# A three-layer graph network: layer 2's twelve dense blocks in three teams of four instead of four teams of three

## The chip, the cores and the metric

The kernel runs on one core of one Trainium2 chip. The time is the device time of one execution in microseconds; the median of three executions of the kernel before is 1999.56 us (1996.38 to 2002.89). All views come from one further execution that the hardware profiler recorded.

## The reference

A graph of 6250 nodes and 100,000 edges, with a self-loop at every node, goes through three graph convolutions (256 to 512, 512 to 512, 512 to 256 columns), each followed by a relu; the result is added to the input and normalized by rows.

```python
deg = segment_sum(ones, dst)              # with the self-loops
norm_edge = rsqrt(deg)[src] * rsqrt(deg)[dst]
for W, b in ((W1, b1), (W2, b2), (W3, b3)):
    msg = (h @ W)[src] * norm_edge[:, None]
    h = relu(segment_sum(msg, dst) + b)
out = layernorm(x + h)
```

## The kernel before

The nodes are cut into 50 blocks of 125 (`Q`). The edges come sorted by destination, so each block has one run of about 2000 edges. Layer by layer the kernel forms, for each block, the sum of its neighbours' rows (a table in HBM: `tables[i]`), multiplies by the weights, and stores its rows of the next table. A block's sum is formed in one of two ways.

- **Gathered** (`gather`, L1198, and `product`, L1226): GpSimd (POOL) issues 16 indirect DMAs, each of 128 rows (in layer 2 of 512 floats, 256 KB), and one more for each group of ten blocks. VectorE makes one-hot matrices, and 26 matmuls add the rows up in a PSUM bank of `accs` (`sacc`). The rows land in a ring of row buffers; a buffer is free again when the block's sum has used it.
- **Dense**: small integers count how often each source occurs for each destination (`kept`, one byte each). ScalarE (ACT) turns five 125x125 pieces at a time into floats (L969 for teams, L1179 elsewhere), and TensorE (PE) multiplies them with all 50 blocks of the table (L1017 for teams).

In layer 2 blocks 0 to 11 are dense and 12 to 49 gathered. The dense ones go in **teams** (`teams`): a team's blocks share every load of the table. A unit is one table block for one team: two units come by one load (L82 by `load`, a pair of DMAs of 448 and 52 KB into one of three `streamed` buffers, in the profile `parts<-tab`); ACT writes the rounded half (L977) and VectorE (DVE) the rest (L979) into one of three `both_parts`; then PE does two matmuls (one pair) for each member of the team, each member in a PSUM bank of its own (`team_banks`). Teams begin at the end of layer 1, and fill the gap in which layer 2's gathers wait for the last rows of its table.

All of this is one program order, written at build time. For layer 2 the loop over gathers (612 of them, counted as `chunk` in `layer`) issues one gather, then the product that has become due (5 gathers behind its block's last), and then lets every generator that is due go one step. A team's generator does one pair for a step. A finished sum goes through `after2`: DVE scales the bank and adds the block's own row (L1367; the own row is loaded by SyncE's queue, SP, and scaled by ACT at L1238), PE transposes the result into the same bank (L1300), ACT copies it out to `zt2` (L1387), and the bank is free. In the order that copy stands eight gathers behind the sum, and the next block's sum eight gathers behind the copy. Two blocks together then go through W2 (L1413, with ACT's relu at L1424) and W3 (L1433). A team's sum is scaled into a `team_sums` buffer first (L1374) and transposed later into another bank (L1393, copied at L1396); where it can, such a block forms a couple with a gathered one.

All engines work in order. The ring of layer 2 has 30 rows: 10 in `room` (13 less one for each `team_sums` buffer), 14 in pairs, 8 on loan from the place of layer 3's table (two for each of `LOANED`), less two that are set aside. When the teams have 12 units left (`RETURN`), loaned rows are no longer used, and the ring has 22.

PSUM has eight banks. Layer 2 uses `accs[0]` and `accs[1]` in turn for gathered sums, `accs[2]`, `mat_ps` and `smm` for the team, `win_ps` and `str` for everything else, and one for constants.

Of the kernel before, what the change touches and what calls it, by code (L numbers as in the profile page):

```python
# [38 lines left out]
PRODUCTS = sum(c1 - c0 for c0, c1 in WINDOWS)  # L39
RUNS = 8  # L40

LOANED = 4
RETURN = 12
LAG = 5
FIRST_ROWS = 20
# [14 lines left out]
FRONT = 12  # L60
FRONT_AT = 3
EXTRA = 4
TEAM = 3
TEAMS = 4
HOME = 19
MANY = 29
ALONE = 2
# [8 lines left out]
def by_rows(queue, tile_rows, dram_rows, store=False):  # L76

    for s in (slice(0, EVEN), slice(EVEN, Q)):
        if store:
            queue.dma_start(out=dram_rows[s], in_=tile_rows[s])  # L80
        else:
            queue.dma_start(out=tile_rows[s], in_=dram_rows[s])  # L82
# [320 lines left out]
def sorted_path(ctx: ExitStack, tc: tile.TileContext, x, edges, starts, found, wts, biases, room, late, again, out):  # L403
# [42 lines left out]
    mat_bank = ps_mat.tile([P, HID], F32, name="mat_ps")  # L446
    win_bank = ps_mat.tile([P, HID], F32, name="win_ps")
# [8 lines left out]
    held, idle = {}, {}  # L456
# [6 lines left out]
    def take(name, most):  # L463
        while held.get(name, 0) >= most:
            yield 1
        held[name] = held.get(name, 0) + 1
# [309 lines left out]
    wide_rows = [room[:, at:at + HID] for at in range(MW, room.shape[1] - 2 * pair - HID + 1, HID)]  # L776
    team_sums = [wide_rows.pop()[:Q] for _ in range(TEAM)]
    last_rows = [room[:, at:at + C] for at in range(3 * MW, room.shape[1] - C + 1, C)]
# [27 lines left out]
    accs = [ps_sum.tile([P, HID], F32, name=f"sacc{n}") for n in range(3)]  # L806
    mm_bank = ps_sum.tile([P, HID], F32, name="smm")
# [116 lines left out]
    def carved(words):  # L924
        nonlocal cut
        cut += words
        assert cut <= tail.shape[1]
        return tail[:, cut - words:cut]

    RING = 3  # L930
    carved(LOANED * 2 * HID)
    loaned = [wide_tail[:, cut - n * HID:][:, :HID].bitcast(F32) for n in range(2 * LOANED, 0, -1)]
    is_loaned = {id(row) for row in loaned}
    streamed = [carved(2 * HID).bitcast(F32).rearrange("p (b c) -> p b c", b=2) for _ in range(RING)]
    both_parts = [carved(2 * HID) for _ in range(3)]
    on_loan = set()
    team_used = [[carved(-(-2 * PIECE * Q // 4)).bitcast(U8)[:, :2 * PIECE * Q].rearrange("p (k v) -> p k v", v=Q) for _ in range(TEAM)]
                 for _ in range(2)]
    team_pieces = [[carved(PIECE * Q).rearrange("p (k v) -> p k v", v=Q) for _ in range(TEAM)] for _ in range(2)]
    team_banks = [accs[2], mat_bank, mm_bank]  # L940
    couple, waiting = [], []
    teams_done = False
    returning = None
# [1 line left out]
    def teams(groups):  # L945
# [4 lines left out]
        def used_by(g, c):  # L950
            return team_used[(g * CUTS // 2 + c // 2) % 2]
# [5 lines left out]
        def next_counts(g, c):  # L957
            if c + 2 < CUTS:
                fetch_counts(g, c + 2)
            elif g + 1 < len(groups):  # L960
                fetch_counts(g + 1, c + 2 - CUTS)
# [6 lines left out]
        def piece(g, c, n):  # L968
            nc.scalar.copy(team_pieces[(g * CUTS + c) % 2][n], used_by(g, c)[n][:, c % 2 * PIECE:(c % 2 + 1) * PIECE, :])  # L969
            if c % 2 and n == TEAM - 1:  # L970
                next_counts(g, c - 1 + 2)
# [15 lines left out]
        yield 14  # L987
        for n in range(TEAM):
            piece(0, 0, n)
# [99 lines left out]
    def layer(i, width, gathered, dense, after, rows, first=0, spacing=1.0, extras=(), filler=None):  # L1089
# [8 lines left out]
        going = []  # L1098
        fixed = [[at, steps] for at, steps in extras]
        idle.clear()  # L1100
        idle.update(acc=accs[:2] if i == 1 else list(accs), acc_d=[mm_bank, win_bank, mat_bank])
        if i == 0:
            del idle["acc"]
        items = []
# [6 lines left out]
        acc_d = None  # L1111
        if done:
            acc_d = idle["acc_d"].pop(0)
# [13 lines left out]
        def go(chunk):  # L1127
            for item in list(going):
                if item[0] <= chunk + late:
                    wait = next(item[1], None)  # L1130
                    if wait is None:
                        going.remove(item)
                    else:
                        item[0] = chunk + late + min(wait, item[2])

        def need(chunk, name, most):
            nonlocal late
            while held.get(name, 0) >= most:
                late += 1
                go(chunk)  # L1140
            held[name] = held.get(name, 0) + 1

        def sum_bank(name, most):
            nonlocal late
            if i == 0:
                while not common:
                    if early_copy[0]():
                        break
                    late += 1
                    go(chunk)  # L1150
                return common.popleft()
            need(now, name, most)
            return idle[name].pop(0)

        def ended(chunk, b, acc, bank="acc"):

            most = LATE if chunk < total - 2 * KF else 1
            going.append([chunk + late + min((3, SOON, LATE)[i], most), after(b, acc, bank), most])
            for item in going:
                item[2] = most  # L1160
# [4 lines left out]
        def one_hot(b):  # L1165

            hot = hots[b] = onehot.tile([P, PRODUCTS, WIN], F32, name="shot")
            at = 0
            for w, (c0, c1) in enumerate(WINDOWS):
                shape = [P, c1 - c0, WIN]  # L1170
                nc.vector.tensor_tensor(hot[:, at:at + c1 - c0], near_cols[:, w * WIN:(w + 1) * WIN].unsqueeze(1).to_broadcast(shape),
                                        dlo[:, b, c0:c1].unsqueeze(2).to_broadcast(shape), op=ALU.is_equal)
                at += c1 - c0
# [27 lines left out]
        def product(c):  # L1201
            n, b, j = items[c]
            if b is None:
                return
            if j == 2:
                one_hot(b)
            if j == KF - LATE:
                if i == 0 and b >= OWN_FROM:
                    by_rows(nc.sync, own_x[b % 2], tables[0][b * Q:(b + 1) * Q, :])
                if i == 1:  # L1210
                    by_rows(nc.sync, own_row, tables[1][b * Q:(b + 1) * Q, :])
            if j < KF - 1:
                return
            acc = sum_bank("acc", 2 if i == 1 else 3)
            own_product = i == 2 or i == 0 and b < OWN_FROM
            if own_product:
                for h in range(2):
                    nc.tensor.matmul(acc[:, :C], lhsT=ident_r[:Q], rhs=parts[:, b, h * C:(h + 1) * C], start=(h == 0), stop=False)
            hot = hots.pop(b)
            of = [landed.pop((b, k)) for k in range(KF)]  # L1220
            each = of + [of_ten[b // GRP]]
            for k in range(max(c1 - c0 for c0, c1 in WINDOWS)):
                at = k
                for w, (c0, c1) in enumerate(WINDOWS):
                    if c0 + k < c1:
                        nc.tensor.matmul(acc[w * WIN:(w + 1) * WIN, :width], lhsT=hot[:, at], rhs=each[c0 + k],  # L1226
                                         start=(not own_product and k == 0), stop=(c0 + k == c1 - 1))
                    at += c1 - c0
            for row in of:
                if id(row) in is_loaned:  # L1230
                    on_loan.discard(id(row))
                    if returning is not None:
                        continue
                ring.append(row)
            if i == 0 and b >= OWN_FROM:
                nc.scalar.activation(own_x[b % 2], own_x[b % 2], AF.Copy, scale=dinv[:, b:b + 1])
            if i == 1:
                nc.scalar.activation(own_row, own_row, AF.Copy, scale=dinv[:, b:b + 1])  # L1238
            ended(now, b, acc)
# [3 lines left out]
        with tc.manual_schedule():  # L1243
            to_sum = 0
            for chunk in range(total + LAG):
# [18 lines left out]
                while done < until:  # L1264
                    m, k = divmod(done, NB)
                    if k == 0:
# [3 lines left out]
                        acc_d = sum_bank(bank, 3)  # L1270
# [89 lines left out]
    def after2(b, acc, bank):  # L1360
# [10 lines left out]
        else:  # L1371
            yield from take(f"sum{b % TEAM}", 1)
            zs = team_sums[b % TEAM]
            nc.vector.tensor_scalar(zs, acc[:Q], dinv[:, b:b + 1], None, op0=ALU.mult)  # L1374
            free(bank, acc)
            if b >= TEAM * (TEAMS - 1) and acc is not mm_bank:
                wins.append(acc)
            yield SOON
            while now < steps(TEAM * TEAMS) - 2 * KF and (len(couple) != 1 or held.get("turn", 0)):
                yield 1  # L1380
# [27 lines left out]
        for f2 in range(0, KH, each):  # L1408
# [11 lines left out]
            for _ in range(2):  # L1420
                if now < steps(TEAM * TEAMS) - 4 * KF and held.get("acc", 0) < 2 and not any(held.get(f"sum{t}", 0) for t in range(TEAM)):
                    yield 1
# [135 lines left out]

    team_work = teams([every[g * TEAM:(g + 1) * TEAM] for g in range(TEAMS)])
    first = 16  # L1560
# [5 lines left out]
    def last_weights():  # L1566
# [11 lines left out]
    own_row = two.enter_context(tc.tile_pool(name="sown_row", bufs=1)).tile([P, HID], F32, name="own_row")[:Q]  # L1578
    gap = (steps(TEAM * TEAMS) - 100) // (MANY - FEW - EXTRA)
    layer(1, HID, every[TEAM * TEAMS:], [], after2, wide_rows,  # L1580
          extras=[(5, last_weights()), (0, team_work), (20, home())]
# [197 lines left out]
```

## Time and profile before

| | |
|---|---|
| median of 3 executions | 1999.56 us |
| profiled execution, its span | 2010.4 us, 2008.7 us |
| PE, POOL, DVE, ACT busy | 92%, 69%, 45%, 45% of the span |
| first to last gather of layer 2 | 703.5 to 1540.2 us |
| mean of DMA traffic | 217 GB/s over the span |

A matmul counts twice in the trace where the type makes the hardware pass twice. Matmuls overlap, so a PE that is busy is not yet a PE at its peak: paces are read from the starts of successive matmuls. In a row of groups, the part behind the bar is busy us, mean ns of one, then idle time before them and what ended it. The chain of waits gives start, length and what the time went to; a DMA in it counts from its issue to its landing.

### The profile page before, as it was taken

What the parts mean: (1) busy time and instruction counts of PE and PEld (TensorE: products, weight loads), DVE (VectorE), ACT (ScalarE), POOL (GpSimd) and SP (SyncE); (2) the same over time, 40 slices, a digit from 0 to 9 for tenths busy, and PEclk for the clock granted to TensorE, in tenths of its full rate; (3) what the DMA queues carried; (4) which work ended last, traced back from release to release, by engine and by line L of the source; (5) the groups of instructions that cost most, each with busy time, mean ns of one, the idle gap of its engine ahead of it and who ended that gap; (6) DMA issues with size and microseconds to landing.
All of it is one profiled execution on the core that took longest, in us unless ns stands there. A gap on an engine that the chain in (4) does not pass through costs nothing.

```text
span 2008.7 us, 31171 instructions
## 1 busy us (share of the span) xinstructions
PE 1848.8 (92%) x11066; PEld 1251.0 (62%) x11066; DVE 901.2 (45%) x1901; ACT 897.8 (45%) x1614; POOL 1380.0 (69%) x1442
## 2 busy tenths in 40 slices
PE   3389999999998969999999999999988999999996
PEld 2367677667674535666666666666644767677773
DVE  4887777666666323323243223432311334343443
ACT  0677677777775423443243433343212333333331
POOL 2277777677677476777777677775775677777775
PEclk9999999999999989999999999999999999999997
DMA  7555555455559899999999999999986576666663
GB/s 162 168 148 175 154 172 155 149 159 173 152 162 253 214 284 267 297 295 284 294 294 280 290 282 289 290 287 266 279 247 196 138 191 181 190 189 190 187 184 109
DMA packets 197012, 435.75 MB, mean 217 GB/s; under 512 B 44124, under 2 KB 87814, under 8 KB 196845
## 3 DMA queue, kind: packets, MB, share of 16 engines
q0 software_dynamic: 88128, 265.01, 46.0%
q1 hardware_dynamic: 92749, 156.71, 28.5%
q10 hardware_dynamic: 15968, 11.92, 2.4%
q8 instruction: 89, 1.46, 0.3%
q14 instruction: 78, 0.64, 0.1%
HBM read 378.83 MB, written 54.66 MB: 216 GB/s over the span
## 4 chain that ended last, share of the span: by engine, by line
PE 73%; DMA 13%; DVE 4%; issue 3%; ACT 2%; POOL 1%; SPq 1%; ACTq 0%; DVEq 0%; POOLq 0%
PE sacc L1226 13%; PE mat_ps L1279 8%; PE sacc L1279 7%; PE win_ps L1279 7%; PE smm L1279 6%; PE win_ps L1413 4%; DMA own_row<-tab 4%; DMA parts<-tab 3%; PE sacc L1017 3%; PE mat_ps L1017 3%; PE smm L1017 3%; DMA row<-tab,ssrc 2%; PE win_ps L1433 2%; PE str L1413 2%; DMA parts<-kept 2%
## 5 line engine op out<-in xcount | busy, mean ns | idle before, releaser
L1198 POOL DMA_INDIRECT row<-tab,ssrc x780 | 754.1, 967 | 273.6 <-issue 162.1
L1198 POOL DMA_INDIRECT room<-tab,ssrc x484 | 467.6, 966 | 174.0 <-issue 97.7
L1179 ACT CAST piece<-room 125x625 fp32r<-125x625 uint8 x416 | 299.8, 728 | 250.9 <-PE mat_ps L1279 76.2
L1226 PE MATMUL sacc<-row,shot 128*32 128x512 f32 (+1 forms) x1786 | 290.4, 510 | 20.9 <-DMA row<-tab,ssrc 17.6
L1226 PE MATMUL sacc<-room,shot 128*32 128x256 f32 (+1 forms) x1506 | 278.6, 489 | 21.9 <-DMA room<-tab,ssrc 21.5
L833 DVE TENSOR_TENSOR room<-near_cols,slots 128x625 bf16<-128x625 f32 (+2 forms) x390 | 289.6, 802 | 11.9 <-PE sacc L905 7.7
L979 DVE TENSOR_TENSOR parts<-parts 125x512 fp32r<-125x512 f32 x200 | 136.4, 690 | 332.6 <-ACT parts L977 306.8
L977 ACT CAST parts<-parts 125x512 fp32r<-125x512 f32 x200 | 121.8, 620 | 165.5 <-DMA parts<-tab 78.3
L1279 PE MATMUL sacc<-parts,piece 125*125 125x512 f32 x600 | 186.3, 428 | 0.0
L1279 PE MATMUL mat_ps<-parts,piece 125*125 125x512 f32 x700 | 185.0, 406 | 0.0
L1226 PEld LDWEIGHTS sacc<-row,shot 128*32 128x32 f32 x1786 | 86.1, 111 | 133.0 <-issue 74.8
L1017 PE MATMUL sacc<-parts 125*125 125x512 f32 x400 | 145.5, 440 | 18.4 <-ACT parts L977 14.8
L1279 PE MATMUL smm<-parts,piece 125*125 125x512 f32 x605 | 156.7, 405 | 2.7 <-ACT piece L1179 2.1
L1198 POOL DMA_INDIRECT parts<-tab,ssrc x128 | 126.0, 984 | 47.6 <-issue 26.8
L1279 PE MATMUL win_ps<-parts,piece 125*125 125x512 f32 x600 | 150.2, 400 | 0.0
L1226 PEld LDWEIGHTS sacc<-room,shot 128*32 128x32 f32 x1506 | 84.5, 112 | 103.8 <-issue 50.3
L1179 DVE CAST piece<-room 125x625 fp32r<-125x625 uint8 x85 | 43.4, 511 | 229.5 <-PE smm L1279 75.5
L1279 PEld LDWEIGHTS mat_ps<-parts,piece 125*125 125x125 f32 x700 | 123.8, 186 | 31.8 <-issue 6.5
L1017 PE MATMUL smm<-parts 125*125 125x512 f32 x400 | 138.5, 428 | 0.3 <-ACT room L867 0.3
L1017 PE MATMUL mat_ps<-parts 125*125 125x512 f32 x400 | 138.5, 428 | 0.0
L905 PEld LDWEIGHTS <-room 128*125 128x125 bf16 x650 | 88.1, 140 | 79.5 <-issue 27.9
L1367 DVE SCALAR_TENSOR_TENSOR szs<-sacc,sdinv,own_row 125x512 f32<-125x512 f32 x38 | 28.5, 750 | 231.1 <-PE sacc L1226 143.6
(358 smaller groups left out, 2975.0 us busy)
## 6 DMA issues: line engine op xcount, KB each, us to landing
parts<-tab SPq DMA_DIRECT2D x105, 448.0 KB
kept<-room SPq DMA_DIRECT2D x29, 683.6 KB
room<-kept SPq DMA_DIRECT2D x29, 683.6 KB
tab<-st SPq DMA_DIRECT2D x62, 224.0 KB
row<-tab,ssrc POOLq DMA_INDIRECT x780
own_row<-tab SPq DMA_DIRECT2D x38, 224.0 KB
parts<-kept SPq DMA_DIRECT2D x60, 136.7 KB
room<-tab,ssrc POOLq DMA_INDIRECT x484
```

Of the source, the lines that this page charges most:

```text
L833: nc.vector.tensor_tensor(out, near_cols[:, :shape[2]].unsqueeze(1).to_broadcast(shape), numbers.unsqueeze(2).to_broadcast(shape), op=ALU. ...
L905: nc.tensor.matmul(bank[:Q, len(pair) * 256:][:, :G * NB], lhsT=hot_lo, rhs=hot_key, start=True, stop=True)
L977: nc.scalar.copy(to[:, :HID], row)
L979: nc.vector.tensor_sub(to[:, HID:], row, to[:, :HID].bitcast(F32))
L1017: nc.tensor.matmul(team_banks[n][:Q], lhsT=team_pieces[(g * CUTS + k // PIECE) % 2][n][:, k % PIECE, :], rhs=both_parts[u % 3][:, h * HID: ...
L1179: convert(piece, made_or_read[:, c * PIECE:(c + 1) * PIECE, :])
L1198: nc.gpsimd.indirect_dma_start(out=row, out_offset=None, in_=tables[i], in_offset=bass.IndirectOffsetOnAxis(ap=at, axis=0))
L1226: nc.tensor.matmul(acc[w * WIN:(w + 1) * WIN, :width], lhsT=hot[:, at], rhs=each[c0 + k], start=(not own_product and k == 0), stop=(c0 + k ...
L1279: nc.tensor.matmul(acc_d[:Q], lhsT=got[done // PIECE][:, k % PIECE, :], rhs=parts[:, k], start=(k == 0), stop=(k == NB - 1))
L1367: nc.vector.scalar_tensor_tensor(zs, acc[:Q], dinv[:, b:b + 1], own_row, op0=ALU.mult, op1=ALU.add)
L1413: nc.tensor.matmul(h_ps[:, f, :], lhsT=w2_sb[:, k, (f2 + f) * P:(f2 + f + 1) * P], rhs=zt2[:, k, :wide], start=(k == 0), stop=(k == KH - 1))
L1433: nc.tensor.matmul(u_ps[:, h, :], lhsT=ht2[:, k, h * Q:(h + 1) * Q], rhs=w3_sb[:, k, :], start=(k == 0), stop=(k == KH - 1))
```

## The change

Four numbers and two lists change. `TEAM` and `TEAMS` go from 3 and 4 to 4 and 3, so the same twelve blocks are dense. The team's fourth bank is `accs[1]`, so gathered sums have `accs[0]` alone. The second pair of `team_pieces` and `team_used` buffers that a fourth member needs comes from the room that `LOANED` = 2 instead of 4 sets free, four rows of the ring; and a fourth `team_sums` buffer takes one more. The ring has 25 rows, and 21 when the loan is returned.

```diff
-LOANED = 4
+LOANED = 2
-TEAM = 3
-TEAMS = 4
+TEAM = 4
+TEAMS = 3
@@ sorted_path
-    team_banks = [accs[2], mat_bank, mm_bank]
+    team_banks = [accs[1], accs[2], mat_bank, mm_bank]
@@ layer
-        idle.update(acc=accs[:2] if i == 1 else list(accs), acc_d=[mm_bank, win_bank, mat_bank])
+        idle.update(acc=accs[:1] if i == 1 else list(accs), acc_d=[mm_bank, win_bank, mat_bank])
@@ product, in layer
-            acc = sum_bank("acc", 2 if i == 1 else 3)
+            acc = sum_bank("acc", 1 if i == 1 else 3)
```

Up to the third gathered sum of layer 2, PE's order is the same in kind. Behind the fourth (block 15) it differs. On PE, from the end of that sum on, before the change (`sacc_934` to `sacc_936` are the three `accs`; `room` at L1393 is a team's sum; L905 are matmuls that count for layer 3):

```order
L1017 MATMUL sacc_936<-parts 125x512 x2
L1017 MATMUL mat_ps<-parts 125x512 x2
L1393 MATMUL win_ps<-ident_r,room 128x125 x4
L1017 MATMUL smm<-parts 125x512 x2
L1017 MATMUL sacc_936<-parts 125x512 x2
L905 LDWEIGHTS hot_pair_6533
L905 MATMUL str<-hot_pair_6533 125x250
L1300 MATMUL sacc_935<-ident_r,szs 128x125 x4
L1017 MATMUL mat_ps<-parts 125x512 x2
L905 LDWEIGHTS hot_pair_6533
L905 MATMUL str<-hot_pair_6533 125x250
L1017 MATMUL smm<-parts 125x512 x2
```

And with the change:

```order
L1017 MATMUL mat_ps<-parts 125x512 x2
L1017 MATMUL smm<-parts 125x512 x2
L1017 MATMUL sacc_935<-parts 125x512 x2
L1017 MATMUL sacc_936<-parts 125x512 x2
L905 LDWEIGHTS hot_pair_6517
L905 MATMUL str<-hot_pair_6517 125x250
L1300 MATMUL sacc_934<-ident_r,szs 128x125 x4
L1017 MATMUL mat_ps<-parts 125x512 x2
L905 LDWEIGHTS hot_pair_6517
L905 MATMUL str<-hot_pair_6517 125x250
L1017 MATMUL smm<-parts 125x512 x2
L1017 MATMUL sacc_935<-parts 125x512 x2
```

A unit now has four pairs, in four banks, and the first team, which ended before this place, ends some 50 gathers later: its transposes (L1393) are gone from here, and so are those of W2's runs that belonged to them. Up to the fifth sum there are 16 pairs in both; instructions of L1413 are 16 before and 8 now, of L1393 8 and none.

On ACT, from the copy of the same block's transposes on, before:

```order
L1387 COPY room<-sacc_935 128x4x125
L867 CAST room<-str 125x2x50x5
L1424 ACTIVATE room<-win_ps,b_sb 128x250 x2
L977 CAST parts<-parts 125x512
L1238 ACTIVATE own_row<-own_row,sdinv 125x512
L1396 COPY room<-win_ps 128x4x125
L977 CAST parts<-parts 125x512
L867 CAST room<-str 125x2x50x5
L977 CAST parts<-parts 125x512
```

And with the change:

```order
L1387 COPY room<-sacc_934 128x4x125
L977 CAST parts<-parts 125x512
L867 CAST room<-str 125x2x50x5
L977 CAST parts<-parts 125x512
L1424 ACTIVATE room<-win_ps,b_sb 128x250 x2
L1238 ACTIVATE own_row<-own_row,sdinv 125x512
L977 CAST parts<-parts 125x512
L969 CAST parts<-parts 125x625 x2
L867 CAST room<-str 125x2x50x5
```

The copy of the team's transposes (L1396) is gone from here, the copy at the head reads the one bank that gathered sums now have (`sacc_934`, before `sacc_935` in turn with it), and the scaling of the next own row (L1238) stands behind it, and ahead of the next copy, as before.

## The prediction

> **What bounds the kernel now.** I read stages first, then what each engine waits for, then the chain. The first view is the busy time of the engines by stage of layer 2 (columns: window, its length, then busy us and count of PE, PEld, DVE, ACT, POOL, then the granted clock, the DMA share and GB/s).
>
> ```profile
> 703.00:760.00 57.00, 40.35 (x172) 19.23 (x174) 11.45 (x22) 14.79 (x26) 42.25 (x43) 0.85 1.00 283
> 760.00:827.00 67.00, 60.99 (x327) 39.99 (x320) 26.14 (x46) 24.27 (x46) 45.62 (x49) 0.97 1.04 276
> 827.00:1403.00 576.00, 566.02 (x3223) 372.43 (x3226) 186.86 (x354) 216.76 (x401) 408.11 (x416) 0.99 1.03 288
> 1403.00:1541.00 138.00, 126.28 (x750) 73.15 (x747) 32.84 (x72) 30.14 (x64) 104.02 (x106) 0.98 0.85 252
> 1541.00:2008.00 467.00, 437.20 (x2650) 317.81 (x2642) 174.86 (x501) 157.08 (x261) 326.66 (x339) 0.96 0.63 172
> ```
>
> In 827 to 1403 both PE (566 of 576 us) and the DMA engines (1.03) look full, so I ask which one waits. Busy time of matmuls overlaps, so I count them: the next four rows are that stretch for line 1017 (the teams' matmuls), 1226 (sums over gathered rows), 1413 (W2) and 1433 (W3), in this order; then come their paces, two rows of PE's timeline and four of the chain of waits, and the longest of six rows of PE's waits there (total, times, longest us).
>
> ```profile
> 827.00:1403.00 576.00, 251.77 (x838) 150.03 (x838) 0.99 1.03 288
> 827.00:1403.00 576.00, 163.83 (x1356) 44.34 (x1360) 0.99 1.03 288
> 827.00:1403.00 576.00, 126.83 (x544) 101.44 (x544) 0.99 1.03 288
> 827.00:1403.00 576.00, 68.26 (x288) 53.45 (x288) 0.99 1.03 288
> 869.22 0.63 PE L1017 MATMUL mat_ps<-parts 125*125 125x512 f32 x2
> 869.68 0.62 PE L1017 MATMUL smm<-parts 125*125 125x512 f32 x2
> 850.38 6.14 PE sacc L1226 x52
> 933.38 1.69 PE win_ps L1413 x8
> 834.47 1.73 PE win_ps L1433 x8
> 1402.93 6.14 PE sacc L1226 x52
> PE sacc L1017 <- ACT parts L977: 6.4, 3, 3.4
> ```
>
> A pair of team matmuls starts every 0.46 us (869.22, 869.68): 838/2 x 0.46 = 193. A gathered block's sum has 52 records in 6.14: 1356/52 x 6.14 = 160. Eight records of W2 take 1.69: 544/8 x 1.69 = 115; of W3 1.73: 288/8 x 1.73 = 62. Together 530 us, without the transposes and the counting matmuls; and the waits that the last row heads come to 9.9 us (6.4, 1.5, 0.8, 0.5, 0.5, 0.2) of 576. **PE is the bound from 827 to 1403**, and the change takes nothing from it there. POOL confirms it: it waits for PE.
>
> ```profile
> L1198 POOL DMA_INDIRECT row<-tab,ssrc x196 | 193.6, 988 | 76.2 <-issue 39.6 <-PE sacc L1226 25.6 <-DMA room<-tab,ssrc 4.0
> 1404.18 0.94 POOL L1198 DMA_INDIRECT room<-tab,ssrc  x1 [10.83 <-PE sacc L1226]
> 1405.43 0.95 POOL L1198 DMA_INDIRECT room<-tab,ssrc  x1 [0.31 <-issue]
> 1539.25 0.94 POOL L1198 DMA_INDIRECT row<-tab,ssrc  x1 [0.30 <-PE sacc L1226]
> 1566.13 0.94 POOL L1198 DMA_INDIRECT room<-tab,rest  x1 [25.94 <-DMA tab<-st]
> ```
>
> A gather costs POOL 1.25 us (1404.18 to 1405.43). After 1404 POOL has one gather behind the other until 1539: 106 of them (stage row) in 136 us, 1.28 each. **POOL is the bound of the tail**, and it starts there when the ring loses its eight loaned rows and POOL waits 10.83 us for a sum on PE. Behind it 26 us pass until layer 3 gathers (1566.13).
>
> The front, 703 to 827, is bound by neither: PE has 101 of 124 us and a low clock. PE's waits of 700 to 760, one row of 760 to 860, and the places:
>
> ```profile
> PE sacc L1017 <- ACT parts L977: 8.4, 5, 5.0
> PE sacc L1226 <- DMA room<-tab,ssrc: 4.8, 2, 4.7
> PE sacc L1300 <- DVE szs L1367: 3.2, 1, 3.2
> 746.35 0.63 PE L1017 MATMUL smm<-parts 125*125 125x512 f32 x2
> 752.00 1.51 PE L1017 MATMUL sacc<-parts 125*125 125x512 f32 x2 [5.03 <-ACT parts L977]
> 753.32 1.05 PE L1017 MATMUL mat_ps<-parts 125*125 125x512 f32 x2
> 754.17 1.05 PE L1017 MATMUL smm<-parts 125*125 125x512 f32 x2
> 715.13 23.23 DMA own_row<-tab
> 738.38 12.80 DMA parts<-tab
> 788.06 0.72 ACT L1238 ACTIVATE own_row<-own_row,sdinv 125x512 f32<-125x512 f32 x1 [16.17 <-DMA own_row<-tab]
> ```
>
> Here the queue of transfers is the bound: an own row lands after 23.2 us, a load of the table for the teams after 12.8; PE's pair at 752.00 waited 5.03 us for the conversion of such a load, and 3.2 us for the own row that landed at 788.
>
> **The change part by part.** *A quarter of the teams' loads.* Four teams read the table in 100 loads (105 with five of another step), three in 75.
>
> ```profile
> parts<-tab SPq DMA_DIRECT2D x105, 448.0 KB
> parts<-tab SPq DMA_DIRECT2D x105, 52.0 KB
> L979 DVE TENSOR_TENSOR parts<-parts 125x512 fp32r<-125x512 f32 x200 | 136.4, 690 | 332.6 <-ACT parts L977 306.8
> L977 ACT CAST parts<-parts 125x512 fp32r<-125x512 f32 x200 | 121.8, 620 | 165.5 <-DMA parts<-tab 78.3
> ```
>
> 25 loads x 500 KB = 12.8 MB go, and with them 50 casts x 0.62 = 31 us of ACT and 50 subtractions x 0.69 = 34.5 us of DVE. Between 827 and 1403 ACT is busy 217 of 576 us and DVE 187, both wait most of the rest, and PE is full: all that falls there is worth nothing. It counts in the front. A converted unit now serves four pairs on PE, 1.84 us instead of 1.38, and three buffers of two units reach a third further. PE's losses there are 8.4 + 4.8 + 3.2 = 16.4 us; bounds are 0 (transfers stay late) and -16 (all gone). The gathers themselves, 1.25 us each on POOL, are nearly as late as PE at 755, so a part of the waits would only change its name. I take **-4**.
>
> Row first, then a rule: after the idle 5.03 us pairs start 0.85 us apart (753.32, 754.17) instead of 0.46, and the stage's clock is 0.85. The Trainium skill, TensorE: Matmul & The Clock Gate, in HAM oscillation, says that an idle gap of over some 3.4 us halves PE's clock until it has been busy again; by that rule a wait shortened below it gains the slow pairs too, here three of them, 1.2 us more than the wait; by the rows alone it gains the wait. The trace agrees at 752.
>
> *Order of W2 and W3.* The teams now end at other places. The order shows that between the fourth and the fifth gathered sum two runs of W2 (four instructions, eight records, 1.69 us each) and two rows of transposes are gone, 3.4 us without the transposes; such runs come later, behind the eighth to tenth sum. Counted with the paces above, the 25 blocks from the fifth sum on hold the same work within 1 us, and two runs of W2 move behind the teams' end, where PE has 12 us to spare (126 of 138). So PE reaches the end of its bound stretch that much earlier. Against it: shorter blocks come near POOL's own 16 x 1.25 = 20.0 us. I take **-3**, bounds 0 and -5.
>
> *Ring.* From 30 rows to 25 (four loaned, one more kept for a team's sum), and after the return from 22 to 21. A sum frees its first row at its start; then POOL must issue 32 - 25 = 7 gathers (8.8 us) and the last must land before the next sum can end. With the landing of 4 to 8 us that the chain shows (the 7.44 below) this is at most 17 of the 20 to 22 us of a block: no wait, cost **0**. In the tail the loan returns 12 gathers earlier and POOL is held one gather sooner: **+1** (1.25), bounds 0 and +7, the last if it is held once more at a landing of
>
> ```profile
> 1539.25 7.44 DMA row<-tab,ssrc
> 682.20 8.26 DMA row<-tab,ssrc
> ACT own_row L1238 <- DMA own_row<-tab: 129.9, 30, 16.2
> ```
>
> 7.44 us. *End of layer 1.* PE's order is the same; the last gather there lands after 8.26 us among the teams' loads, four of which go: **-1**, bounds 0 and -6 (2 us for a landing without company). *One bank for gathered sums.* The next sum stands eight gathers, 10 us, behind ACT's copy that frees the bank, and that distance is the cover: **0**; without it see rival (c).
>
> **Sum**: -4 - 3 + 0 + 1 - 1 = -7 us against the profiled execution's 2010.4 (span 2008.7): 2003. The median of the runs shown is 1999.56, 10.8 below that execution, so the forecast there is **1992.5**; the bounds sum to -27 and +7. What a measurement of this kernel can tell from no change is about 0.3%, 6 us.
>
> **Rivals.** *(a) Nothing is left, 1997.5.* PE-bound work takes up what the front gains: moved W2 falls where POOL is just behind, the transfers in the front stay late (500 KB in eight gathers instead of six is 63 KB instead of 83 beside each gather's 256, only 6% less), and the tail gives 1 to 2 us back. For it: a full PE and POOL's 136 us tail, neither touched. Sum: -1 to -3.
>
> *(b) Transfers are the bound, 1966.* If the DMA share of 1.03 is what paces PE, 12.8 MB at 288 GB/s is 44 us; POOL's tail of 136 us can't shrink, so some 34 remain. Against it: PE's waits for transfers in 827 to 1403 are under 10 us. The limit would show as PE idle.
>
> *(c) One bank is slower, 2012.* Until now a second bank took the next sum while ACT held the first. ACT works in order, and the scaling of the own row stands ahead of the copy: it waited 30 times for the transfer, 129.9 us in all, 4.3 on average, 16.2 at most. The copy stands 10 us ahead of the sum that needs the bank; only a transfer that lands over 10 us late holds PE. If ten of the 30 came 2 us too late for that, PE would lose 20 us: 1992.5 + 20 = 2012. Against it: fewer loads run ahead of own rows on SP, and PE's transposes before it wait for the same row today. The Trainium skill, PSUM — Partial Sum Buffer, in PSUM bank collisions raise a hardware error, speaks against the change: two engines may not touch one bank and quadrant at once, so with one bank copy and next sum can only follow one another. No run here shows what that costs.
>
> **How the numbers follow.** Forecast (1985 to 1995) 0.5; (a) 0.3; (b) 0.08; (c), with the ring's +7, 0.12. The range leaves out most of (b) and the far half of (c): 1979 to 2006. Faster by over 0.3%: most of the forecast and (b), 0.53; within: (a) and the forecast's edge, 0.35; slower: 0.12.
>
> **What would show it.** Loads of the table fall from 105 to 80, PE's waits for conversions in the first 120 us of layer 2 from 8.4 to under 4, and the granted clock there rises above 0.85. The sixth or seventh gathered sum comes about 8 us earlier relative to layer 2's first gather, the eighth to tenth block give back the moved W2, and from the first to the last gather 837 us become about 831. POOL's 10.83 us wait at the loan's return shrinks to about half. I am wrong if PE's sums show waits on ACT's copy, if POOL's waits for sums in 830 to 1400 (25.6 us in the first of its rows) grow by 10 us (the ring), or if the PE-bound stretch gets shorter by more than 10 us (b).

## The result, and the profile after

| | before | after |
|---|---|---|
| median, beside each other on one chip | 2001.22 us (4 runs, 1996.38 to 2005.4) | 1974.95 us (4 runs, 1973.03 to 1979.28) |
| profiled execution, its span | 2010.4, 2008.7 us | 1974.0, 1972.3 us |
| first to last gather of layer 2 | 836.7 us | 806.9 us |

The ratio is 0.9862, with a 95% interval of 0.9833 to 0.9891: 26 us faster, where 7 were forecast; the time lies under the range (1979 to 2006). A later set of runs (e13 below) gives 0.9856 [0.9832, 0.988]. The two profiled executions lie 36 us apart, ten more than the medians, since that of before is one of its slower ones. So differences between the two traces show where the time went; how much a cause is worth comes from the timed runs.

The stages of layer 2 in the changed kernel's profile (window, length, then busy us and count of PE, PEld, DVE, ACT and POOL, granted clock, DMA share, GB/s), in the windows of the prediction:

```profile
703.00:760.00 57.00, 44.72 (x210) 22.34 (x209) 13.31 (x27) 15.45 (x27) 42.85 (x45) 0.91 1.02 289
760.00:827.00 67.00, 65.49 (x366) 40.95 (x365) 22.89 (x41) 25.00 (x45) 51.04 (x53) 1.00 1.03 283
827.00:1403.00 576.00, 574.01 (x3309) 380.26 (x3308) 170.02 (x327) 195.40 (x361) 421.37 (x432) 1.00 0.97 278
1403.00:1541.00 138.00, 125.75 (x731) 79.33 (x731) 29.63 (x71) 38.41 (x80) 89.09 (x94) 0.99 0.75 225
```

PE is busy 574 us of the 576 instead of 566, and does 3309 matmuls there instead of 3223. The DMA share fell from 1.03 to 0.97: transfers no longer fill their engines all the time. These are all of PE's waits in the changed kernel, first from 700 to 830 and then (the last row) from 830 to 1400:

```profile
PE sacc L1226 <- DMA room<-tab,ssrc: 4.9, 7, 1.5
PE sacc L1226 <- issue: 3.9, 1, 3.9
PE sacc L1300 <- DVE szs L1367: 3.3, 1, 3.3
PE sacc L1226 <- DMA row<-tab,ssrc: 1.4, 1, 1.4
PE sacc L1226 <- DMA parts<-tab,ssrc: 0.2, 1, 0.2
PE sacc L1226 <- DMA room<-tab,ssrc: 2.0, 3, 1.4
```

No wait for a conversion (L977) is left in either stretch; before they came to 8.4 and 6.4 us. The 6.4 us are three waits, and two of them make up 5.6 us. These rows show both in the kernel before, each behind the wait of ACT that caused it:

```profile
1001.47 1.14 ACT L977 CAST parts<-parts 125x512 fp32r<-125x512 f32 x2 [9.89 <-DMA parts<-tab]
1002.13 1.52 PE L1017 MATMUL sacc<-parts 125*125 125x512 f32 x2 [3.40 <-ACT parts L977]
1171.59 0.72 ACT L1238 ACTIVATE own_row<-own_row,sdinv 125x512 f32<-125x512 f32 x1 [12.76 <-DMA own_row<-tab]
1172.87 0.49 PE L1017 MATMUL sacc<-parts 125*125 125x512 f32 x1 [2.24 <-ACT parts L977]
```

The first is a late load of the table. The second is a late own row, behind which the conversion stands in ACT's order. In the changed kernel PE waits 2.0 us in all from 830 to 1400, and no gathered sum waits for ACT's copy out of its bank (L1387).

One view that the prediction does not use is the chain of waits inside the stretch from 827 to 1403, summed by line. Before, and then after:

```profile
by line: PE sacc L1226 22.5%; PE win_ps L1413 12.5%; PE mat_ps L1017 8.6%; PE sacc L1017 8.3%; PE smm L1017 8.1%; PE win_ps L1433 7.9%; DMA parts<-kept 6.6%; DMA parts<-tab 6.1%; DMA own_row<-tab 4.8%; PE str L1413 4.2%; PE sacc L1300 1.4%;
917.85 13.60 DMA parts<-tab
```

```profile
by line: PE sacc L1226 26.0%; PE sacc L1017 15.7%; PE win_ps L1413 12.4%; PE smm L1017 7.9%; PE mat_ps L1017 7.8%; PE str L1413 5.9%; PE win_ps L1433 5.8%; PE str L1433 4.2%; DMA room<-tab,ssrc 2.8%; PE sacc L1300 1.9%; POOL row L1198 1.8%;
```

Before, 17.5% of that chain (6.6 + 6.1 + 4.8; 101 us of 576) runs through loads of counts, loads of the table and own rows, in pieces of 13 us like the one at 917.85. After, none of the three is among the chain's larger parts: what is left is PE, and 2.8% of gathered rows. Those 101 us are not lost time, though. The load of 917.85 lands at 931, and PE has no wait between 861 and 998: the chain says which transfers the work runs through, and PE's own rows say where that cost something.

The table gives us between events of the trace (starts of gathers, L1198, and of the 38 gathered sums, 52 records of L1226 each). "To sum 4" counts from layer 2's first gather; "31 to last" is from the 31st sum to layer 2's last gather; "boundary" from that gather to layer 3's first. The e-numbers are the experiments below. e10 has the order, loads and ring of the kernel before up to layer 2's last gathers, so beside the first row it shows how far two executions of the same work differ.

| kernel | to sum 4 | 4 to 5 | 5 to 31 | 31 to last | boundary |
|---|---|---|---|---|---|
| before | 98.0 | 25.4 | 575.8 | 136.4 | 26.9 |
| after | 87.6 | 18.2 | 561.4 | 138.7 | 21.8 |
| after, once more (e13) | 86.9 | 18.2 | 561.6 | 140.3 | 21.9 |
| e1 | 88.1 | 23.6 | 564.3 | 134.7 | 26.8 |
| e2 | 95.9 | 23.6 | 577.5 | 135.8 | 27.2 |
| e3 | 94.9 | 25.4 | 585.8 | 135.6 | 21.8 |
| e4 | 97.7 | 24.4 | 577.4 | 135.6 | 23.1 |
| e5 | 89.1 | 18.2 | 565.7 | 140.0 | 26.8 |
| e6 | 91.1 | 24.7 | 580.6 | 140.3 | 25.7 |
| e9 | 88.5 | 23.6 | 573.1 | 134.6 | 22.0 |
| e10 | 94.2 | 25.0 | 576.3 | 135.1 | 23.9 |
| e11 | 87.1 | 23.6 | 562.3 | 134.7 | 21.9 |
| e12 | 88.8 | 23.6 | 571.2 | 134.0 | 21.8 |

Before to after: -10.4, -7.2, -14.4, +2.3, -5.1, and -1.2 from the first gather's start (703.5 to 702.3). These are the 36 us of the profiles. Against e10 the first of them is only -6.6, so the front's gain is known to some 4 us; the stretch of sums 5 to 31 comes out the same (-14.9).

### The profile page after: what moved, and what is told of

The parts are those of the page before. It is cut to its first block, busy times and chain, and to the rows that moved or that the text cites. A ratio compares the mean times of both kernels' runs of the same rounds, so it can differ in the third digit from the quotient of the medians.

```text
span 1972.3 us, 30841 instructions
## 1 busy us (share of the span) xinstructions
PE 1830.9 (93%) x11066; PEld 1246.1 (63%) x11066; DVE 868.1 (44%) x1851; ACT 870.5 (44%) x1564; POOL 1378.2 (70%) x1442
## 4 chain that ended last, share of the span: by engine, by line
PE 75%; DMA 11%; POOL 4%; issue 3%; DVE 2%; ACT 1%; SPq 0%; POOLq 0%; DVEq 0%; ACTq 0%
PE sacc L1226 13%; PE sacc L1279 7%; PE mat_ps L1279 7%; PE win_ps L1279 6%; PE smm L1279 6%; PE sacc L1017 5%; DMA room<-tab,ssrc 5%; PE win_ps L1413 4%; DMA row<-tab,ssrc 4%; PE mat_ps L1017 3%; PE smm L1017 3%; PE str L1413 2%; POOL room L1198 2%; PE sacc L1331 2%; PE win_ps L1433 2%
## 5 line engine op out<-in xcount | busy, mean ns | idle before, releaser
L1198 POOL DMA_INDIRECT row<-tab,ssrc x830 | 800.1, 964 | 285.1 <-issue 182.5
L1198 POOL DMA_INDIRECT room<-tab,ssrc x490 | 475.2, 970 | 161.4 <-issue 97.9
L1226 PE MATMUL sacc<-row,shot 128*32 128x512 f32 (+1 forms) x1862 | 310.2, 517 | 16.2 <-DMA row<-tab,ssrc 11.0
L1226 PE MATMUL sacc<-room,shot 128*32 128x256 f32 (+1 forms) x1506 | 284.7, 484 | 24.2 <-DMA room<-tab,ssrc 23.5
L833 DVE TENSOR_TENSOR room<-near_cols,slots 128x625 bf16<-128x625 f32 (+2 forms) x390 | 289.6, 802 | 11.5 <-PE sacc L905 7.3
L979 DVE TENSOR_TENSOR parts<-parts 125x512 fp32r<-125x512 f32 x150 | 102.4, 690 | 234.8 <-ACT parts L977 228.9
L1017 PE MATMUL sacc<-parts 125*125 125x512 f32 x600 | 190.0, 424 | 2.3 <-ACT room L867 2.0
L1226 PEld LDWEIGHTS sacc<-row,shot 128*32 128x32 f32 x1862 | 91.4, 110 | 129.9 <-issue 86.8
L1226 PEld LDWEIGHTS sacc<-room,shot 128*32 128x32 f32 x1506 | 84.3, 111 | 111.2 <-issue 44.4
L905 PEld LDWEIGHTS <-room 128*125 128x125 bf16 x650 | 88.3, 141 | 78.6 <-issue 26.6
L1017 PEld LDWEIGHTS sacc<-parts 125*125 125x125 f32 x600 | 106.6, 186 | 37.8 <-issue 10.6
L1279 PEld LDWEIGHTS smm<-parts,piece 125*125 125x125 f32 x605 | 108.7, 187 | 30.7 <-issue 4.2
L867 ACT CAST room<-sacc 125x500 uint8<-125x500 f32 (+1 forms) x143 | 101.2, 723 | 58.1 <-PE sacc L905 45.4
L1279 PEld LDWEIGHTS win_ps<-parts,piece 125*125 125x125 f32 x600 | 108.6, 185 | 28.4 <-issue 3.7
```

The source lines that it names most:

```text
L833: nc.vector.tensor_tensor(out, near_cols[:, :shape[2]].unsqueeze(1).to_broadcast(shape), numbers.unsqueeze(2).to_broadcast(shape), op=ALU. ...
L867: nc.scalar.copy(place[:, :, u * G:(u + len(ms)) * G].rearrange("p k (t r) -> p t k r", r=G), counted_in.rearrange("p (t v) -> p t v", t=2 ...
L905: nc.tensor.matmul(bank[:Q, len(pair) * 256:][:, :G * NB], lhsT=hot_lo, rhs=hot_key, start=True, stop=True)
L979: nc.vector.tensor_sub(to[:, HID:], row, to[:, :HID].bitcast(F32))
L1017: nc.tensor.matmul(team_banks[n][:Q], lhsT=team_pieces[(g * CUTS + k // PIECE) % 2][n][:, k % PIECE, :], rhs=both_parts[u % 3][:, h * HID: ...
L1198: nc.gpsimd.indirect_dma_start(out=row, out_offset=None, in_=tables[i], in_offset=bass.IndirectOffsetOnAxis(ap=at, axis=0))
```

## The experiments

Times stand beside those of the kernel before on the same chip, in three sets of runs. Sets are compared by their ratios.

**Which part of the teams' traffic counts: e1, e2, e8.** Starting from the kernel before, a quarter of the loads, of the conversions, or of both is left out; the order on every engine is otherwise that of before.

```diff
@@ load, in e1 and e8
-            if 2 * p < len(units):
+            if 2 * p < len(units) and p % 4 != 3:
@@ conversion, in e2
-            if u < len(units):
+            if u < len(units) and u % 4 != 3:
@@ conversion, in e8
-            if u < len(units):
+            if u < len(units) and u // 2 % 4 != 3:
```

> The kernel before, in its own order, but every fourth load of the table for the teams is not issued (25 of 100, 12.8 MB); the conversions still run, on what the buffer held, so this leaves out a quarter of the teams' input. Theory T (it is the traffic: 25 loads less let own rows and loads land in time, so that PE neither stands nor falls to half clock): most of the 26 us, 1975 to 1985 us, the waits of PE for conversions in 700 to 1400 (15 us before) under 3 us, POOL's time from first to last gather of layer 2 under 820 us (837 before). Theory O (it is the order, the later end of the first team and the moved runs of W2): 1995 to 2003 us, no change. Theory C (it is the work of ACT and DVE): 1995 to 2003 us.

> The kernel before with all its loads, but every fourth unit of the teams is not converted (50 of 200 casts on ACT, 50 of 200 subtractions on DVE go); the matmuls use what the buffer held, so a quarter of the conversions is left out. Theory C (ACT's and DVE's work, in whose queues the wait for an own row holds the conversions): 1975 to 1985 us. Theory T (traffic): the loads still come late, but a fourth unit does not wait for its own, so up to 5 us of the 15 us of waits go: 1993 to 2002 us.

> The kernel before with neither every fourth load nor the conversions that belong to it (25 loads, 50 casts, 50 subtractions left out; the matmuls use what the buffers held). If the gains of fewer loads (ratio 0.9899) and of fewer conversions (0.9964) are two things they add: 0.986, 1976 to 1982 us. If both are one, the late load, then 0.989 to 0.991, 1983 to 1988 us.

Measured: e1 1985.87 against 2005.87, ratio 0.9899 [0.9883, 0.9916], -20 us. e2 0.9964 [0.9946, 0.9981], -7 us. e8 1982.32 against 2003.36, 0.9894 [0.9864, 0.9924], -21 us. So the loads are worth 20 us with all conversions still there, and taking the conversions too adds nothing that can be told from zero. That fits one cost, a unit that is converted late because its load is late; two costs that add up (0.986) lie at the edge of e8's interval and are not ruled out. ACT's waits from 703 to 1403 show what 25 loads less do, in the kernel before and then in e1 (total, times, longest):

```profile
ACT own_row L1238 <- DMA own_row<-tab: 129.4, 28, 16.2
ACT parts L977 <- PE smm L1017: 66.3, 27, 8.0
ACT parts L977 <- DMA parts<-tab: 64.5, 16, 15.3
```

```profile
ACT parts L977 <- PE smm L1017: 125.9, 46, 9.9
ACT own_row L1238 <- DMA own_row<-tab: 49.1, 16, 6.4
ACT parts L977 <- DMA parts<-tab: 23.2, 3, 14.6
```

Most loads now arrive before PE is done with the buffer (ACT waits 125.9 us for PE and 23.2 for loads), and own rows, whose number e1 doesn't touch, are waited for 49.1 us instead of 129.4. With 25 loads less, the other loads and the own rows come earlier. PE's waits on conversions from 830 to 1400 fall from 6.4 us to

```profile
PE sacc L1017 <- ACT parts L977: 0.8, 1, 0.8
```

yet the stretch of sums 5 to 31 is 11.5 us shorter in e1's trace: more than the wait that went. The whole gain falls at the two places shown above. Counted from layer 2's first gather, e1 leads the kernel before by 11.7 us at the twelfth sum, by 18.3 from the fourteenth to the twentieth, and by 23.3 from the 21st to the 31st; in between, the two run at the same pace. Other kernels in teams of three with all loads wait for conversions at the same two places: e2 for 3.58 and 2.41 us, e10 for 2.03 and 5.05. PE's rows around both places, before and then in e1 (window, length, busy us and count, granted clock, DMA share, GB/s):

```profile
978.00:1030.00 52.00, 48.14 (x275) 0.93 1.04 294
1160.00:1190.00 30.00, 27.29 (x160) 0.94 1.04 283
```

```profile
978.00:1030.00 52.00, 51.24 (x292) 1.00 1.00 288
1160.00:1190.00 30.00, 30.00 (x185) 1.00 1.05 292
```

Behind each wait PE's granted clock falls too. As an estimate, 0.07 of 52 us and 0.06 of 30 us are 5.4 us of clock; with the two waits (5.6 us) that makes 11.0, where 11.5 were measured.

**Is it the distance or the bytes: e4.** The kernel before with four `streamed` buffers instead of three (two rows of the ring go for it), so that loads are issued earlier.

```diff
-LOANED = 4
+LOANED = 3
-    RING = 3
+    RING = 4
```

> The kernel before with four buffers instead of three for the teams' loads, so each load is issued two units (six pairs on PE) earlier, with the same traffic; the place comes from the loan (two rows of the ring less, 28). If late landing of the teams' loads is the cause and an earlier issue cures it: 1980 to 1992 us. Theory T as bandwidth (the transfers as a whole are too many, own rows and gathers too land late): 1995 to 2003 us, the waits of PE for conversions fall but those for gathered rows rise.

Measured: 2003.52, ratio 0.9989 [0.997, 1.0008]: nothing. ACT's and PE's waits of e4 (703 to 1403, and from 830 on):

```profile
ACT own_row L1238 <- DMA own_row<-tab: 177.5, 25, 23.8
ACT parts L977 <- PE smm L1017: 78.4, 35, 9.9
```

```profile
PE sacc L1300 <- DVE szs L1367: 5.8, 3, 5.4
PE sacc L1017 <- ACT parts L977: 2.3, 2, 1.6
```

ACT's waits for loads of the table are down from 64.5 to 7.1 us, and own rows are later for it (177.5 us instead of 129.4), so from 830 on PE waits mostly for DVE's scaling with the own row (5.8 us) instead of for conversions; from 700 to 830 it still waits 9.0 us for conversions. Loads issued earlier only change places with other transfers, which speaks for the amount as the limit. The Trainium skill, DMA: Bandwidth & Descriptors, in Issuing engines are not separate DMA queues, says that transfers of all issuers run on the same DMA engines and interleave; that agrees with loads of SP delaying its own rows here, and with e1. One rival stays open: loads and own rows also share SP's queue, which issues in order, and no run keeps the bytes and takes the loads out of that queue.

**The opposite direction: e5 and e6.** e6 is the changed kernel with 25 loads of 500 KB put back, into a buffer that nothing reads; the room for that buffer costs two rows of the ring, so e5 is its control, with the two rows less alone.

```diff
@@ in e5 and e6
-LOANED = 2
+LOANED = 1
@@ in e6 alone
+    spare = carved(2 * HID).bitcast(F32).rearrange("p (b c) -> p b c", b=2)
@@ load, in e6 alone
+                if p % 3 == 2:
+                    by_rows(nc.sync, spare, tables[1][k * Q:(k + 2) * Q, :].rearrange("(b p) c -> p b c", p=Q))
```

> The changed kernel with one pair of rows less on loan (ring 23 instead of 25, 21 after the return as before); it is the control of the next run, which needs their place. If the ring costs nothing until a sum has to wait for a landing of over 10 us: 0.986 of the kernel before, 1972 to 1982 us. If the ring is short already: 5 us or more slower, 1980 to 1990 us, with POOL's waits for sums up.

> The changed kernel with the traffic of before: behind every third load of the table the same 500 KB are loaded once more into a buffer that nobody reads (25 loads, 12.8 MB); order, conversions, bank as in the changed kernel, ring as in its control. Theory T (traffic as such): the 20 us of the kernel with fewer loads are lost again, 1992 to 2000 us, ratio 0.993 to 0.998, PE's waits in the first 130 us of layer 2 and its half-clock stretches are back. If it is the distance by which a load is issued ahead (a unit of four lasts longer) or the order: ratio 0.986 to 0.989, 1974 to 1980 us.

Measured: e5 1986.0, ratio 0.9917 [0.9888, 0.9945]; e6 2014.89, 1.0068 [1.0037, 1.0099]. The loads put back cost 29 us, more than the 20 that theory T had: with them, and with a ring of 23 rows instead of 30, the new grouping is slower than the kernel before. The stage, ACT's wait and PE's wait of e6 (its lines are three higher, L1303 is L1300):

```profile
827.00:1403.00 576.00, 558.15 (x3178) 369.23 (x3171) 162.87 (x315) 193.72 (x360) 400.15 (x411) 0.99 0.99 281
```

```profile
ACT own_row L1241 <- DMA own_row<-tab: 191.6, 24, 22.1
```

```profile
PE sacc L1303 <- DVE szs L1370: 15.7, 4, 8.2
```

PE's 574 busy us are 558 again, and it waits for own rows. e5 also shows that a ring of 23 rows isn't free: 11 us separate it from the changed kernel (0.9862), of which its trace has 5.0 at the boundary and 4.3 in sums 5 to 31.

**Bank, ring and grouping: e3, e9, e11, e12, e13.** e3 is the kernel before with the change's bank and ring, e9 is e8 with them (all of the change but the grouping in fours); e11 is e8 with the smaller ring and still two banks; e12 is e9 again, beside e11 and the changed kernel (e13) on one chip.

```diff
@@ in e3, e9, e11 and e12 (e9, e11 and e12 with both edits of e8 too)
-LOANED = 4
+LOANED = 2
@@ in e3, e9 and e12
-        idle.update(acc=accs[:2] if i == 1 else list(accs), acc_d=[mm_bank, win_bank, mat_bank])
+        idle.update(acc=accs[:1] if i == 1 else list(accs), acc_d=[mm_bank, win_bank, mat_bank])
-            acc = sum_bank("acc", 2 if i == 1 else 3)
+            acc = sum_bank("acc", 1 if i == 1 else 3)
```

> The kernel before with four teams of three and all loads, but with the price of the change alone: one bank for gathered sums, and four rows of the ring less (26, and 22 after the return). Forecast's price: the bank 0, the ring 0 to +1: 1998 to 2006 us. Rival (c): 2010 us or more, with waits of PE's sums for ACT's copy out of the bank in the trace. If a shorter ring itself helps, because fewer gathers are under way at once: 1990 us or less.

> The last one with the one bank for gathered sums and the shorter ring too (26 rows, 22 after the return): everything of the change but the grouping in fours, so teams end where they ended. If the order of W2 and W3 is worth the 3 us of the forecast: 3 to 6 us slower than the changed kernel, 1977 to 1982 us. The step from layer 2 to 3 should be 22 us and not 27, since the shorter ring holds the load of layer 3's counts back until the last gathers have landed. If the single bank costs something in the old order (3.3 us of waits on ACT's copy in the kernel with only bank and ring changed), up to 1987 us.

> The kernel before without every fourth load of the table for the teams, without the conversions of these units (the teams multiply old values there), and with 26 rows of ring instead of 30 (LOANED 2); gathered sums keep two banks. Beside the next kernel it prices the single bank in the old grouping, beside the changed kernel it prices grouping and bank together. If the bank costs the 3 to 8 us that PE's waits on the copy in the earlier one-bank kernel suggest (3.4 us of waits and what follows them): 0.986 to 0.988 here and 0.990 to 0.992 for the next. If the bank costs nothing: the same ratio for both, about 0.990.

> The last kernel with one bank for gathered sums: all that the change does, but for the grouping of twelve blocks in fours (the same kernel as e9, beside the changed kernel this time). Theory that traffic is nearly all of the gain: within 3 us of the changed kernel, ratio to before 0.986 to 0.988. Theory that the other order of W2, W3 and transposes is worth a part of its own: 6 to 12 us slower than the changed kernel, 0.990 to 0.992.

> The changed kernel itself, on the same chip as the three others, as the reference for them: 0.986 as at first; with the profile a second look at where PE and POOL wait in layer 2.

Measured: e3 0.9997 [0.9983, 1.0011]; e9 0.9911 [0.9882, 0.994]. Beside 2003.2 us of before, the last three:

| | us | ratio | step |
|---|---|---|---|
| e11: loads, conversions, smaller ring | 1979.11 | 0.9873 [0.9851, 0.9895] | -24.1 |
| e12: and one bank | 1982.49 | 0.9887 [0.9866, 0.9908] | +3.4 |
| e13: and teams of four | 1974.15 | 0.9856 [0.9832, 0.988] | -8.3 |

Of the 29.1 us, 24.1 come without another grouping. The bank's +3.4 is no more than the runs scatter (e11 1975 to 1981, e12 1978 to 1990), but e12's waits of PE from 830 to 1400 show where one bank can cost time:

```profile
PE sacc L1226 <- ACT room L1387: 3.4, 5, 0.7
PE sacc L1017 <- ACT parts L977: 2.9, 1, 2.9
PE win_ps L1393 <- ACT room L1424: 1.8, 2, 1.4
```

Five of 38 sums wait up to 0.7 us for ACT's copy in the grouping by threes, none in fours. The Trainium skill, Perfetto Trace Analysis, in Matmuls, says that independent groups should go through different banks so that one is emptied beside the next; here one bank shows 3.4 us of such waits in one order and none in the other. The grouping's step is -8.3 beside e12, and 10 us for e9 against the first pair of runs; either is uncertain by some 6 us. In the traces it lies between sums 4 and 5 (23.6 to 18.2, where the runs of W2 left) and in sums 5 to 31 (571.2 to 561.6). But e11, in threes with two banks, has 562.3 there: in that stretch teams of four only take back what one bank costs teams of three. Bank and grouping together, e13 beside e11, are -5.0 us, which is not clear of zero either. The traces don't decide it, since e12's is its slowest execution (1989.64) and e11's its fastest (1975.35).

**The boundary: e10.** In both traces a load of layer 3's counts goes out near layer 2's last gathers. On SP's queue of the kernel before (start, us):

```profile
1539.25 11.89 SPq L82 DMA_DIRECT2D room<-kept  x4
```

The same load on SP's queue of the changed kernel, and behind it that kernel's last gather in the chain of waits:

```profile
1513.33 1.61 SPq L82 DMA_DIRECT2D room<-kept  x4
```

```profile
1508.28 3.91 DMA row<-tab,ssrc
```

Before, the load starts with the last gather, which then takes the 7.44 us that the prediction shows; after, the ring's other rotation holds the load back until the last sum, and the gather lands in 3.91. e10 is the kernel before with that load issued by ACT behind its last copies:

```diff
-        by_rows(nc.sync, used[len(there) % 2].rearrange("p k v -> p (k v)"), kept[b])
+        by_rows(nc.scalar if chunk == 6 else nc.sync, used[len(there) % 2].rearrange("p k v -> p (k v)"), kept[b])
```

> The kernel before, with one load changed: the counts of layer 3's second dense block (room<-kept after the last gather of layer 2) are issued by ACT, behind its last copies of layer 2, and not by SP, which issued them beside the last gathers. Nothing else. Theory (the shorter boundary of the changed kernel, 21.8 instead of 26.9 us between the last gather of layer 2 and the first of layer 3, comes from this load alone, which the ring's other rotation holds back until the last sum): the last gather lands in about 4 us instead of 7.4, the boundary falls to about 22 us, the ratio to before is about 0.9975. Rival (the boundary is shorter because there is less work of PE and ACT behind the last sum): the boundary stays at 26 to 27 us, ratio 1.000.

Measured: 2005.59 against 2003.2, ratio 1.0011 [0.9993, 1.0029], and a boundary of 23.9. The load was late only in part, as ACT's queue in e10 and, behind it, the last gather in e10's chain show:

```profile
1534.82 0.33 ACTq L82 DMA_DIRECT2D room<-kept  x1
1541.47 0.55 ACTq L82 DMA_DIRECT2D room<-kept  x1
```

```profile
1534.56 5.69 DMA row<-tab,ssrc
```

The gather lands in 5.69 us instead of 7.44, between the two theories, and the time doesn't show it. That the rotation is worth 5 us to the changed kernel is what the traces suggest: all with `LOANED` = 2 have 21.8 to 22.0, the others 23.1 to 27.2, though all have 21 or 22 rows once the loan is returned. No timed run proves it.

## Why the prediction was wrong

**The step that failed** is "PE is the bound from 827 to 1403, and the change takes nothing from it there", and with it, for loads and conversions, "all that falls there is worth nothing". The term for a quarter of the loads was counted in the front alone and put at nothing in this stretch. Instead the stretch gave 14.4 us in the trace (575.8 to 561.4); with the loads alone gone (e1) it gave 11.5, and with 25 put back (e6 against e5) it lost 14.9. PE was the bound for most of the stretch, as predicted, but at two places a late load or own row stopped it through ACT, for 3.40 and 2.24 us, and its clock fell behind each.

Rival (b) named the resource, and I gave it 0.08 because "PE's waits for transfers in 827 to 1403 are under 10 us". That number was right; wrong was to take it as too small to matter. The 6.4 us of waits for conversions were time that fewer loads could remove, and each wait costs more than itself. The size of (b) was off as well: it let the transfers pace the whole stretch and took 34 us, but PE had only 10 us of idle time there (566 of 576) and becomes the bound itself. ACT's waits would have overstated it too: in the changed kernel ACT still waits 94.0 us for own rows, and from 700 to 1400 PE never waits for a conversion.

Part of the loss was pace, not idleness. The teams' matmuls (L1017) in the stage from 703 to 760, before and then after:

```profile
703.00:760.00 57.00, 23.70 (x76) 15.31 (x75) 0.85 1.00 283
```

```profile
703.00:760.00 57.00, 23.63 (x97) 17.24 (x95) 0.91 1.02 289
```

The same busy time holds 97 matmuls instead of 76. The prediction priced the slow pairs at one place (1.2 us) and left them out of its sum; a term made from waits alone leaves out the slow matmuls behind each wait. The wait of 2.24 us, shorter than the 3.4 us that the prediction names, was followed by a lower clock as well. That the clock makes the whole difference in the front is argued, not shown.

**The other steps.** *Front*, -4 within 0 to -16: -10.4 in the trace (-6.6 against e10), -9.9 with the loads alone gone (e1). The mechanism was right (waits for conversions 8.4 to none, clock 0.85 to 0.91), the size was not: I let the gathers take up three quarters of it, but PE's waits for gathered rows hardly grew from 700 to 830 (5.0 to 6.5 us). *Order of W2 and W3*, -3 within 0 to -5: between sums 4 and 5 -7.2, of which e1 has 1.8 without any new order, so about -5 at this place. What came back was far more than two runs of W2: the lead over before falls from 26.0 us at the eighth sum to 6.3 at the twelfth, and is 33 at the 31st. The order's net worth isn't shown; with the bank it is the -5.0 of e13 beside e11, uncertain by some 6. *Ring*, 0: POOL's waits for sums from 830 to 1400 didn't grow (25.6 before; the row below is the changed kernel's), but two rows less cost time in e5. *Tail*, +1: +2.3; POOL's 10.83 us wait at the loan's return is gone altogether, not halved. *End of layer 1*, -1: -1.2, which may be luck, since the first gather starts anywhere from 702.8 to 704.5 in e2, e3 and e10, which have the loads of before; the 2 us for a landing without company, from which its bound came, stand in no row (the shortest landing shown is 3.91). *One bank*, 0: no wait on L1387 in the changed kernel, so rival (c) fell; the waits appear in the order of threes (e12). *The boundary* had no term: -5.1 in the trace, its cause not settled by e10.

```profile
POOL row L1198 <- PE sacc L1226: 21.8, 18, 6.2
```

Of the signs that were to show it, the loads (105 to 80), the conversions' waits and the clock in the front came as named. The sixth and seventh sums came 16.9 and 23.6 us earlier from layer 2's first gather, not 8, and first to last gather fell to 807 us, not 831. The last sign, a PE-bound stretch shorter by more than 10 us, was to mean (b), and it came: transfers did bind, though at two places and not throughout.

## What to carry to other kernels

Where two resources are both nearly full in a stretch, a bound engine that is busy 98% of the time can still lose time to the other. Look up each wait of the bound engine one by one, follow it through the engine that feeds it (here ACT) to the transfer behind it, and read the granted clock around it: the price is the wait plus the slow work that follows. The chain of waits tells which transfers are involved, but its share of the time is not the loss. When loading earlier only moves the delay to other transfers, as in e4, look for fewer bytes: loads that more consumers can share.

## What the runs showed of the hardware that was not expected

With gathers of rows, loads and stores together, this core's transfers moved 276 to 289 GB/s in the stages shown with a share of 0.99 to 1.04. Near that point waits answer steeply: 25 loads of 500 KB less, 3% of the 436 MB that the whole kernel moves, changed ACT's waits for own rows from 129.4 to 49.1 us (e1), and the time by 20 us one way (e1) and 29 the other (e6 against e5).

A wait of PE of 2.24 us, with 0.30 and 0.17 us more right behind it, was followed by a lower granted clock (0.94 over the 30 us around 1172.87, and 1.00 in e1, where the wait is gone).
